# Two of the six channel sums in the first image's spectral mixings: on TensorE with the identity and a ScalarE copy, instead of a VectorE reduction

## The chip, the cores and the metric

The kernel runs on one core of one Trainium2 chip. The metric is device microseconds of one execution of the whole program. A core has a matrix engine (TensorE, PE in the profile; its weight loads are listed apart, as PEld), three elementwise engines (VectorE or DVE, ScalarE or ACT, GpSimd or POOL) and queues for transfers, of which SyncE (SP) issues most here. TensorE reads the on-chip memory SBUF and writes accumulator banks (PSUM) of 128 partitions by 512 f32 numbers; VectorE and ScalarE read both.

## The reference, cut to what matters

Eight images of 8 channels by 256 x 256 pixels, in f32. Each image goes through a group normalisation, a lift to 4 groups of 10 channels, four spectral layers, two pointwise layers and a residual sum, and then a second normalisation with a 3 x 3 dilation. A spectral layer is

```python
xf = jnp.fft.rfft2(x).reshape(Bb, G, WID, Hh, Wf)            # G = 4, WID = 10
lo = jnp.einsum('bgixy,gioxy->bgoxy', xf[:, :, :, :M1, :M2], w1c)   # M1 = M2 = 12
hi = jnp.einsum('bgixy,gioxy->bgoxy', xf[:, :, :, Hh - M1:, :M2], w2c)
out_ft = out_ft.at[:, :, :, :M1, :M2].set(lo)
out_ft = out_ft.at[:, :, :, Hh - M1:, :M2].set(hi)
h1 = jnp.fft.irfft2(out_ft, s=(Hh, Ww))
h = swish(h1 + gconv1x1(h))                                  # no swish in the last layer
```

Only 24 x 12 frequencies are kept. At each of them and in each group, ten complex input channels `i` are multiplied by a complex weight and summed into ten output channels `o`. This product and sum over `i` is the mixing, and the change is in its sums.

## The kernel before, in words

One image after the other is worked on, and in each the layers 0 to 3. Of a layer the order is: the spectrum of the layer's input (`spectrum_x` for layer 0, `spectrum_h` for the others), the mixing (`mix`), the rows of the inverse transform (`rows_even`, `rows_odd`), and then `layer`, which goes through eleven chunks of the image: each `burst` adds the inverse transform along the columns and the pointwise convolution in a bank, ScalarE takes it through the swish into `h`, and VectorE and TensorE (`turn`, `transform`, `gather`) already make the forward transform for the next layer. The pointwise layers at the end of an image (its head: `first`, `second`) are cut into 128 steps, which are set between the pieces of the next image's layers at the places where the generators `yield` a text such as "fc". In the first image there is no head to put there: its `mix` runs with nothing between. Layer 0 of the next image is prepared by the generator `start(b + 1)` while layer 3 of this one runs; for the first image it runs ahead of all else.

The order of instructions on TensorE, VectorE, ScalarE and SyncE is the order of the program's text (a manual schedule); each engine works its queue in that order, and a framework adds semaphore waits where one engine needs another's data or its buffer. So an instruction that waits holds up all that stand behind it on the same engine.

In `mix` the partitions are frequencies (24 rows by 4 sets, in 128 partitions) and three values of `k` cover the rest. There are 12 steps, n = 0 to 11: `k = n // 4`, and `k2` is 0 for the real and 1 for the imaginary part of the spectrum. At an even n VectorE multiplies (L420) the weights `sw[k]`, 4 groups x 20 (ten outputs, real and imaginary) x 10 input channels, by the spectrum `bt`, and writes 800 products a partition into `pr`. At an odd n it sums (L423) the ten input channels of each into 80 numbers of `S0` or `S1`. `pr` lies in the third plane of the buffer `turned`, in one half for k2 = 0 and in the other for k2 = 1, so n = 2, 6 and 10 write the same half. When all twelve are done, L438 (odd layers) or L441 and L442 (even layers) form the real and imaginary differences and sums `fs`. TensorE folds these (L464) into the banks of `ps_four`, VectorE copies them to `fz`, and TensorE makes the rows (L496 in even layers, L518 in odd ones), which ScalarE (L215) and VectorE (L217) copy to `zt` for the bursts.

Accumulator banks come from two tags: "one" (`ps_a`, one bank, two buffers in turn) and "tri" (three banks, two buffers). The weights of the three `k` are loaded by the SP queue (L409) into three buffers `sw`, those of the next layer as soon as this layer's multiplications have freed them; in layer 3 the next image's x is loaded by the same queue at n = 2 (L78). `ident` is a 128 x 128 identity that the kernel already has for its transposes (L324).

Other lines that are spoken of: L318 and L331, matmuls of the first image's spectrum, the second with a full 128 x 128 weight; L325 and L334, the VectorE copies before and after L331; L390 and L401, the matmuls of `spectrum_h`; L600, L603 and L606, the matmuls of a burst (L600 in layer 0, where the input has 6 rows of each 32; L603 in the other layers).

Of the kernel before, what the change touches and what calls it, by code (L numbers as in the profile page):

```python
# [12 lines left out]
AF = mybir.ActivationFunctionType  # L13
# [9 lines left out]
WID = 10  # L23
# [23 lines left out]
def fno_dilate_kernel(ctx: ExitStack, tc: tile.TileContext, a: dict, out: bass.AP):  # L47
    nc = tc.nc
    mm = nc.tensor.matmul
# [9 lines left out]
    def ps_a(name):  # L59
        return ps.tile([128, 512], F32, tag="one", bufs=2, name=name)  # L60

    def ps_tri(name):
        return ps.tile([128, 3, 512], F32, tag="tri", bufs=2, name=name)

    def ps_four(name):
        one, tri = ps_a(f"{name}_0"), ps_tri(f"{name}_1")
        return one, tri, [one] + [tri[:, i, :] for i in range(3)]

    def part(i):
        return slice(32 * i, 32 * i + 32)  # L70
# [5 lines left out]
    def load_x(b):  # L76
        for i in range(2):
            nc.sync.dma_start(turned[:, i], a["xw"][b, :, i])  # L78
# [10 lines left out]
    ident = const.tile([128, 128], F32, tag="ident", name="ident")  # L89
# [79 lines left out]
    p = ps_tri("p_wc")  # L169
    for g in range(G):  # L170
        mm(p[32 * g : 32 * g + 6, 0, :32], fc0x[part(g), :], wt[part(g), 0, g, :], start=True, stop=True)
    for i in range(2):
        for r in range(4):
            mm(p[part(r), 1, NO * G * i : NO * G * (i + 1)], fc0c[:, i, :], wbd[:, NO * r : NO * (r + 1), :],
               start=True, stop=True)
# [236 lines left out]
    def mix(b, l, out_):  # L412

        s = [sb.tile([128, 3, 2, WID, G], F32, tag=f"S{i}", bufs=1, name=f"S{i}_{b}_{l}") for i in range(2)]
        bt, sw = out_["bt"], out_["sw"]
        for n in range(12):
            k, k2 = n // 4, n // 2 % 2
            pr = turned[:, 2, 1024 * k2 : 1024 * k2 + 800].rearrange("p (g m i) -> p g m i", g=G, i=WID)
            if n % 2 == 0:
                nc.vector.tensor_tensor(  # L420
                    pr, sw[k], bt[:, k2, k].unsqueeze(2).to_broadcast([128, G, 2 * WID, WID]), ALU.mult)
            else:
                nc.vector.tensor_reduce(  # L423
                    s[k2][:, k].rearrange("p s o g -> p (s o) g"),
                    pr.rearrange("p g m i -> p m g i"), AX.X, ALU.add,
                )
            if l == 0:
                if n % 2:
                    yield
            elif n not in (0, 2, 6, 10):  # L430
                yield {1: "fc", 4: "fC", 7: "fC", 9: "fC"}.get(n, "f")
            if n == 2 and l == 3 and b + 1 < n_img:
                load_x(b + 1)
        for i, (x, y, op) in enumerate((
                (s[0][:, :, 0], s[1][:, :, 1], ALU.subtract), (s[0][:, :, 1], s[1][:, :, 0], ALU.add),
                (s[1][:, :, 1], s[0][:, :, 0], ALU.subtract))):
            if l % 2:
                nc.vector.tensor_tensor(fs2[:, :, i].rearrange("p g k o -> p k o g"), x, y, op)  # L438
                continue
            three = [t[:, :, :9].rearrange("p k (r o) g -> p k r (o g)", r=3) for t in (x, y)]  # L440
            nc.vector.tensor_tensor(fs[:, 0:3, i].rearrange("p r k o g -> p k r (o g)"), *three, op)  # L441
            nc.vector.tensor_tensor(fs[:, 3, i, :, 0], x[:, :, 9], y[:, :, 9], op)  # L442
        yield "fc"

        if l % 2:
            src, cols = fs2.rearrange("p g i k o -> p g i (k o)"), fz2
            nc.vector.memset(fz2[:, :, 25], 0.0)
            if l == 1:
                nc.vector.tensor_copy(fz2[:, :, 24], cz1)
            else:  # L450
                nc.vector.memset(fz2[:, :, 24], 0.0)
        else:
            src, cols = fs.rearrange("p r i k o g -> p r i (k o g)"), fz.rearrange("p o g c -> p (o g) c")
            if l == 2:
                nc.vector.tensor_copy(fz[:, :, :, 24], cz[:, 1])
                nc.vector.memset(fz[:, :, :, 25], 0.0)
            else:
                nc.vector.tensor_copy(fz[:, :, :, 25], cz[:, 2])
        n_f = 6 * cols.shape[1]
        one, tri, banks = ps_four(f"p_f_{b}_{l}")  # L460
        for term in range(2):
            for r in range(4):
                for q in range(4):
                    mm(banks[q][part(r), :n_f], fold[part(q), term, :],  # L464
                       src[part(q), r, term : term + 2].rearrange("p t x -> p (t x)"),
                       start=term == 0, stop=term == 1)
        if l == 0:
            mr = out_["mr"]
            nc.vector.tensor_tensor(dc[:, 0:1], mr[:, 0:1], mr[:, 1:2], ALU.mult)
            out_["wcn"] = sb.tile([128, 32], F32, tag="wcn", bufs=1, name=f"wcn_{b}")  # L470
            nc.vector.tensor_scalar(out_["wcn"], wc, mr[:, 1:2], None, ALU.mult)
            for r in range(4):
                mm(one[part(r), n_f : n_f + NO * G], dc, wm[:, NO * r : NO * (r + 1), :], start=True, stop=True)
        nc.vector.tensor_copy(
            cols[:, :, 6:24].rearrange("p x (q c) -> p q c x", q=3),
            tri[:, :, :n_f].rearrange("p q (c x) -> p q c x", c=6))
        nc.vector.tensor_copy(
            cols[:, :, 0:6].rearrange("p x c -> p c x"), one[:, :n_f].rearrange("p (c x) -> p c x", c=6))
        if l == 0:
            nc.vector.tensor_tensor(  # L480
                fz[:, :, :, 24], one[:, n_f : n_f + NO * G].rearrange("p (o g) -> p o g", o=NO), cz[:, 0], ALU.add)
# [204 lines left out]
    def start(b, out_):  # L686
        if b < n_img:
            if b == 0:
                out_["sw"] = [load_sw(0, k) for k in range(3)]
            yield from spectrum_x(b, out_)  # L690
            yield from mix(b, 0, out_)
# [11 lines left out]
    def layers(b, stored, d, then, ahead):  # L703

        for l in range(4):
            if l > 0:
                yield from spectrum_h(b, l, d)  # L710
                yield from mix(b, l, d)
            yield from rows_odd(b, l, then) if l % 2 else rows_even(b, l)
            yield from layer(b, l, d, stored, then, ahead)
        yield "stored"
        yield from rest(b, then)
# [429 lines left out]
```

## Time and profile before

| | |
|---|---|
| median of 3 runs | 3658.42 us (3650.33, 3658.42, 3659.02) |
| profiled execution | 3659.15 us, its span 3657.4 us |
| mean granted TensorE clock | 0.977 of full |
| busy: TensorE, ScalarE, VectorE | 3478.5, 2873.7, 2381.7 us |
| L420, products, 192 of them | 188.7 us, 983 ns each |
| L423, sums, 192 of them | 188.9 us, 984 ns each |
| the first image's four mixings (n = 0 to 11) | from 40.45, 123.40, 199.49 and 277.07 us, 11.6 us each |

The 192 products and 192 sums are those of 32 mixings (8 images, 4 layers). The span is the time from the first to the last instruction of one profiled execution; all times in the trace count from its start. A line of the profile gives start and length in us, engine, line in the code, operation, output <- inputs, shape, and in brackets how long the engine had been idle before it and what ended that. A line by source gives the shortest, median and longest duration of the line's instructions in ns.

### The profile page before, as it was taken

How to read it: one execution, taken by the hardware profiler on the slowest of the kernel's cores; microseconds unless marked ns; L12 is line 12 of the kernel's file. 1: busy time of each engine (PE TensorE's matmuls, PEld its weight loads, DVE VectorE, ACT ScalarE, POOL GpSimd, SP SyncE). 2: the span in 40 equal slices, each digit the busy share in tenths (PEclk: the TensorE clock that was granted, in tenths of full speed). 3: DMA queues.
4: the chain of work that ended last, by engine and by line, in shares of the span. 5: the costliest groups of instructions: out<-in, count | busy, mean ns of one | idle time of the engine just before them, and what ended most of it. 6: DMA issues, size and time to landing. Idle time of an engine off the chain costs nothing.

```text
span 3657.4 us, 112630 instructions
## 1 busy us (share of the span) xinstructions
PE 3478.5 (95%) x50872; PEld 1271.2 (35%) x50872; DVE 2381.7 (65%) x3697; ACT 2873.7 (79%) x3035; POOL 117.0 (3%) x202
## 2 busy tenths in 40 slices
PE   5768999999999999999999999999999999999997
PEld 2323333333333333333333333333333333333222
DVE  6776656557775677756776577766777567772443
ACT  2435888888888888887888888888888888889986
POOL 1000000000000000000000000000000000000000
PEclk7878999999999999999999999999999999999998
DMA  3005211442225222271223512254222521225331
GB/s 93 16 15 206 58 47 50 152 121 65 76 87 185 81 60 73 87 226 55 64 60 126 183 56 76 64 166 119 67 76 87 192 81 53 71 70 191 83 84 48
DMA packets 114080, 344.70 MB, mean 94 GB/s; under 512 B 15985, under 2 KB 18481, under 8 KB 98177
## 3 DMA queue, kind: packets, MB, share of 16 engines
q1 hardware_dynamic: 95392, 276.32, 24.9%
q0 software_dynamic: 18208, 61.18, 5.3%
q8 instruction: 400, 6.55, 0.7%
q14 instruction: 80, 0.65, 0.1%
HBM read 213.44 MB, written 123.74 MB: 92 GB/s over the span
## 4 chain that ended last, share of the span: by engine, by line
PE 80%; DVE 13%; ACT 4%; issue 3%; DMA 0%; ACTq 0%; DVEq 0%; POOL 0%; POOLq 0%
PE p_fc L825 21%; PE p_fc L842 21%; PE p_z L606 10%; PE p_d L567 8%; PE p_z L603 8%; PE p_u L585 3%; PE p_z L600 3%; DVE y L851 2%; DVE S L423 2%; DVE turned L420 2%; DVE turned L550 2%; PE p_b L390 1%; DVE turned L381 1%; PE p_g L518 1%; ACT act L826 1%
## 5 line engine op out<-in xcount | busy, mean ns | idle before, releaser
L827 ACT ACTIVATE act<-p_fc 128x1536 f32<-128x1536 f32 x1024 | 1492.0, 1457 | 3.1 <-PE p_fc L825 3.1
L825 PE MATMUL p_fc<-hs,c_w 32*128 32x512 f32 x8192 | 1132.7, 625 | 24.6 <-DVE y L851 10.0
L842 PE MATMUL p_fc<-act,c_w 128*32 128x512 f32 x8192 | 1007.1, 599 | 0.5 <-ACT act L827 0.2
L826 ACT ACTIVATE act<-p_fc 128x512 f32<-128x512 f32 x1024 | 616.0, 602 | 199.7 <-PE p_fc L825 187.6
L550 DVE STREAM_TRANSPOSE turned<-h 128x1024 f32<-128x1024 f32 x528 | 632.6, 1226 | 196.0 <-ACT h L611 195.2
L611 ACT ACTIVATE h<-p_z 128x512 f32<-128x512 f32 (+1 forms) x528 | 512.0, 1021 | 205.8 <-PE p_z L606 205.8
L851 DVE TENSOR_TENSOR y<-p_fc,y 128x512 f32<-128x512 f32 x392 | 267.7, 683 | 526.0 <-PE p_fc L842 526.0
L825 PEld LDWEIGHTS p_fc<-hs,c_w 32*128 32x128 f32 x8192 | 357.9, 184 | 595.0 <-ACT act L826 260.2
L842 PEld LDWEIGHTS p_fc<-act,c_w 128*32 128x32 f32 x8192 | 222.4, 109 | 704.9 <-issue 327.4
L606 PE MATMUL p_z<-c_binv,zt 32*128 32x256 f32 x5632 | 414.2, 408 | 0.1
L606 PEld LDWEIGHTS p_z<-c_binv,zt 32*128 32x128 f32 x5632 | 261.2, 188 | 309.5 <-issue 296.1
L603 PE MATMUL p_z<-h,c_wt 32*32 32x512 f32 x8448 | 358.0, 601 | 7.9 <-ACT act L826 4.2
L567 PE MATMUL p_d<-turned,c_fw 32*32 32x480 f32 (+1 forms) x9216 | 308.0, 539 | 0.6 <-DVE turned L550 0.2
L575 ACT ACTIVATE turned<-p_d 128x1440 f32<-128x1440 f32 x144 | 183.1, 1272 | 89.7 <-PE p_d L567 86.6
L613 ACT ACTIVATE h<-p_z,c_bias 128x512 f32<-128x512 f32 (+1 forms) x176 | 186.6, 1111 | 72.0 <-PE p_z L606 71.8
L215 ACT ACTIVATE zt<-p_g 128x198 f32<-128x198 f32 (+2 forms) x132 | 62.5, 583 | 177.6 <-PE p_g L496 93.7
L423 DVE TENSOR_REDUCE S<-turned 128x80 f32<-128x800 f32 x192 | 188.9, 984 | 5.9
L420 DVE TENSOR_TENSOR turned<-t,B 128x800 f32<-128x800 f32 x192 | 188.7, 983 | 1.1
L567 PEld LDWEIGHTS p_d<-turned,c_fw 32*32 32x32 f32 x9216 | 127.5, 103 | 165.5 <-issue 63.8
L381 DVE STREAM_TRANSPOSE turned<-zt 128x960 f32<-128x960 f32 x96 | 177.1, 1868 | 2.5
L603 PEld LDWEIGHTS p_z<-h,c_wt 32*32 32x32 f32 x8448 | 92.9, 103 | 175.5 <-DVE y L851 48.8
L585 PE MATMUL p_u<-turned,c_stack 128*32 128x480 f32 (+1 forms) x1152 | 136.7, 543 | 7.2 <-DVE turned L574 6.2
(198 smaller groups left out, 1748.2 us busy)
## 6 DMA issues: line engine op xcount, KB each, us to landing
stored<-h SPq DMA_DIRECT2D x88, 1024.0 KB
hs<-stored SPq DMA_DIRECT2D x352, 256.0 KB
t<-in_spw SPq DMA_DIRECT2D x96, 400.0 KB
yin<-y_rows POOLq DMA_DIRECT2D x56, 512.0 KB, 5.1
h<-in_xp SPq DMA_DIRECT2D x352, 48.0 KB
turned<-in_xw SPq DMA_DIRECT2D x16, 1024.0 KB
y<-in_x SPq DMA_DIRECT2D x56, 256.0 KB
y_rows<-y POOLq DMA_DIRECT2D x56, 256.0 KB, 3.9
```

Of the source, the lines that this page charges most:

```text
L420: nc.vector.tensor_tensor(pr, sw[k], bt[:, k2, k].unsqueeze(2).to_broadcast([128, G, 2 * WID, WID]), ALU.mult)
L423: nc.vector.tensor_reduce(s[k2][:, k].rearrange("p s o g -> p (s o) g"), pr.rearrange("p g m i -> p m g i"), AX.X, ALU.add,)
L550: nc.vector.transpose(dst[:, 2 * i : 2 * i + 2], h[:, c, 2 * i : 2 * i + 2].rearrange("p f (s x) -> p f s x", s=2))
L567: mm(banks[q][part(v % 4), : 240 * n], fw8[part(q), v, :], t[part(q), :, :, v, : NBLK * WID], start=v < 4, stop=v >= 4)
L603: mm(o, wt[part(q), l, g, :], h[part(q), c, f, :], start=True, stop=False)
L606: mm(banks[q][:, HW * s : HW * (s + 1)], zt[part(q), 2 * c + s].rearrange("p f o -> p (f o)"), binv[part(q), :], start=False, stop=s == 1)
L611: nc.scalar.activation(dst, src, AF.Silu)
L825: mm(banks[g], w1[part(g), blk, :], hs[k][part(g), :], start=True, stop=True)
L826: nc.scalar.activation(act[:, 0, :], one, AF.Silu)
L827: nc.scalar.activation(act[:, 1:4, :], tri, AF.Silu)
L842: mm(acc[part(g), :], w2[:, g, 15 - rb - i : 47 - rb - i], act[:, g, :], start=i == 0, stop=i == 1)
L851: nc.vector.tensor_tensor(y, sums, y, ALU.add)
```

## The change

Where the image is the first (b = 0), in each of its four layers, the sums at n = 3 and n = 7 (k2 = 1, k = 0 and 1) are no longer made by VectorE. TensorE takes a bank of tag "one" and multiplies the identity, as the stationary weight, by the 80 products of input channel i, for i = 0 to 9, accumulating in the bank; so the bank holds the sum over i. The ten matmuls read `pr` with i fixed, in the order (output, group): successive numbers are 800 bytes apart in g (4 of them) and 40 bytes apart in m (20 of them). ScalarE then copies the 80 numbers to the same place in `S1`. The other four sums of these mixings, and all sums of the other images, stay on VectorE.

```diff
             if n % 2 == 0:
                 nc.vector.tensor_tensor(
                     pr, sw[k], bt[:, k2, k].unsqueeze(2).to_broadcast([128, G, 2 * WID, WID]), ALU.mult)
+            elif b == 0 and n in (3, 7):
+                p = ps_a(f"p_mix_{b}_{l}")
+                for i in range(WID):
+                    mm(p[:, 0:80], ident, pr[:, :, :, i].rearrange("p g m -> p m g"), start=i == 0, stop=i == WID - 1)
+                nc.scalar.activation(
+                    s[k2][:, k].rearrange("p s o g -> p (s o g)"), p[:, 0:80], AF.Copy)
             else:
                 nc.vector.tensor_reduce(
                     s[k2][:, k].rearrange("p s o g -> p (s o) g"),
```

## The prediction

> **What bounds the kernel now.** I read the page first: TensorE (PE) is busy 95% of the span and carries 80% of the chain that ended last. The granted clock in forty slices shows where the change lies: only the first four slices (366 us) and the last are below 9 tenths, and the first image fills nearly those.
>
> ```profile
> PE 3478.5 (95%) x50872; PEld 1271.2 (35%) x50872; DVE 2381.7 (65%) x3697; ACT 2873.7 (79%) x3035; POOL 117.0 (3%) x202
> PEclk7878999999999999999999999999999999999998
> ```
>
> The average says nothing about the first image: there is no earlier image whose head could fill its mixings. So I read the timeline of one of them (layer 1):
>
> ```profile
> 124.42 0.99 DVE L423 TENSOR_REDUCE S<-turned 128x80 f32<-128x800 f32 x1
> 125.33 0.98 DVE L420 TENSOR_TENSOR turned<-t,B 128x800 f32<-128x800 f32 x1
> 126.34 0.99 DVE L423 TENSOR_REDUCE S<-turned 128x80 f32<-128x800 f32 x1
> 127.25 0.98 DVE L420 TENSOR_TENSOR turned<-t,B 128x800 f32<-128x800 f32 x1
> 128.26 0.99 DVE L423 TENSOR_REDUCE S<-turned 128x80 f32<-128x800 f32 x1
> 129.17 0.98 DVE L420 TENSOR_TENSOR turned<-t,B 128x800 f32<-128x800 f32 x1
> ```
>
> VectorE works without a gap, one operation each 0.96 us; of its step n=2 (125.33) the sum n=3 follows at 126.34, and n=6 starts at 129.17. Then the windows of the four mixings (PE, PE loads, VectorE, ScalarE, GpSimd, then granted clock), and of two stretches after them:
>
> ```profile
> 40.45:52.10 11.65, 0.00 (x0) 0.00 (x0) 11.40 (x13) 0.00 (x0) 0.00 (x0) 0.50 0.43 106
> 123.40:135.04 11.64, 0.00 (x0) 0.00 (x0) 11.40 (x12) 0.00 (x0) 0.00 (x0) 0.50 0.23 72
> 277.07:288.71 11.64, 0.00 (x0) 0.00 (x0) 11.40 (x12) 0.00 (x0) 0.00 (x0) 0.50 0.33 139
> 58.39:72.04 13.65, 13.65 (x179) 4.88 (x176) 5.42 (x5) 7.93 (x9) 0.00 (x0) 0.50 0.01 2
> 136.89:140.31 3.42, 2.72 (x104) 2.75 (x112) 1.43 (x4) 0.00 (x0) 0.00 (x0) 0.50 0.02 5
> ```
>
> Two things: VectorE alone sets the mixing's 11.6 us (PE's fold, L464, waits 12.8 us for it), so what is gained or lost there goes straight to the end. And PE stands at half clock in it.
>
> **What a group of the new matmuls costs.** The nearest rows are L331, also a full 128x128 weight, in a stretch at full clock, and L496, 128 weight columns at half clock:
>
> ```profile
> L331 PEld LDWEIGHTS p_a<-c_fw,turned x8: 186/192/192, 34.4 to 35.2; 128*128 128x128 f32 x8
> L331 PE MATMUL p_a<-c_fw,turned x8: 269/269/290, 34.4 to 35.2; 128*128 128x24 f32 x8
> 34.40 0.97 PEld L331 LDWEIGHTS p_a<-c_fw,turned 128*128 128x128 f32 x8 [1.02 <-DVE turned L325]
> 34.41 1.07 PE L331 MATMUL p_a<-c_fw,turned 128*128 128x24 f32 x8 [0.78 <-DVE turned L325]
> L496 PEld LDWEIGHTS p_g<-c_rowg,fz x20: 281/328/332, 54.6 to 57.4; 32*128 32x128 f32 x20
> ```
>
> Four calls in the code leave eight loads and eight matmuls: an f32 matmul is two of each. The eight loads start every (970-192)/7 = 111 ns although each must be followed by its matmul: the loads set the pace, the matmuls hide under them. [...] At half clock a load goes from 186 to 281 ns, 95 more. So a load paces at 111+95 = 206 to 2x111 = 222 ns; I take 215. [...] L390's 48 matmuls of 120 columns, four side by side, took 2.63 us at half clock, 12 rounds of about 200 ns[...]. Our 80 columns then stream in 133 ns cold (67 warm), under the load either way.
>
> A group of ten calls is 20 loads and 20 matmuls: cold 19 x 0.215 + a tail. The tail is 0.29 us for L331 (1.07 - 7 x 0.111); cold and with 80 columns for 24 it grows by 0.10 (load) and 0.11 (133 less 20 ns of stream) to 0.50. G = 4.09 + 0.50 = 4.6 us. Warm: 19 x 0.111 + 0.34 = 2.46 us.
>
> **Is it cold?** [...] being busy isn't enough: from 58.39 to 72.04 PE was busy all the time and stayed at 0.50. There L600 feeds only 6 of each 32 rows. [...] The window from 136.89, mostly L518 at all rows, [...]ended the half clock. The group streams 133 of each 215 ns[...]. I take cold.
>
> **The sum.** Removed, per mixing: two sums of 0.99 us at n=3 and n=7. Added: two groups, and a wait that the diff doesn't show: n=2, n=6 and n=10 write the same half of `turned`, so n=6 waits until the group has read it, and n=10 for the second. Behind n=6 on VectorE everything queues, the fold on PE too. From the end of n=2 (126.31) to n=6 (129.17) it was 2.86 us. Now: 0.05 hand-over to PE (34.35 to 34.40 at L325 to L331) + 4.6 + 0.04 back (35.48 to L334 at 35.51) = 4.69; meanwhile VectorE does n=4 and n=5 in 1.95 us and stands idle 2.7. So +1.83 us a group, eight groups (two in each of four layers): +14.6 us. Bounds: 2.55 warm gives -0.31 a group, -2.5 in all; the strided read below gives +23.6.
>
> Hidden: the copies on ScalarE. Its row for 198 elements is 583 ns on average, so 80 take less; ScalarE has no other work before L215, and n=10 and n=11 (1.95 us) cover the last copy; without that cover it is 0.4 us at most in each mixing. The bank is one of the pair "one", whose earlier readers ended before n=0, and the fold takes it after the copy, much later. ScalarE's function loads keep their number and their place. The loads on the SP queue (next layer's weights, the x of the second image) are issued at the same steps and landed long before their use (x by 282 for 296.7). Nothing in the trace between 52 and 300 us waits for a transfer that would absorb the shift, so all of it passes to the end. The profiled execution was 3659.15 us (span 3657.4), 0.7 above the median: 3659.15 + 14.6 = 3673.8, and from the median 3658.42, 3673.0.
>
> **Rivals.**
> *The clock rises.* If the weight loads count as activity, the first group brings the full clock. For it: PE would be busy without a break for over 4 us. Against it: L606 loads as densely and the bursts at 58 to 72 stayed cold. Groups of 2.46 us: 3655.9. If the clock also held over the 2.7 us from the second group to the fold, layer 0's four bursts would go from 3.98 to 2.24 us (1.09+1.15 as later), another -7.0: 3649, on the other side of no change. The point from which it decides is a group of 2.77 us: shorter gains, longer loses.
> *The strided read slows PE.* The moving columns lie 40 and 800 bytes apart. [...] L390, which reads runs of three, took 2.63 us cold and 1.96 warm, not half; isolated elements are in no row. At 267 ns a matmul, twice the stream, G is 19 x 0.267 + 0.65 = 5.7, +2.95 x 8 = +23.6: 3682. At 200 ns nothing changes cold, but a warm group is then 4.2 us, +11: 3669.
> *It is swallowed.* The runs of before lie at 3650.3 and at 3658.4 to 3659.0. The trace has one window of 3.4 us at half clock in layer 0 of each of the last six images (the first from 788.84 to 792.25), after L600 with its six rows[...]. At up to 1.7 us each, six are up to 10, the size of that step. A luckier phase could give 8 us back: 3665, or with a smaller group 3660.
>
> **How the numbers follow.** Cold, paced by loads: 0.57, 3673, own range 3664 to 3677. Strided read: 0.15, 3669 to 3682. Clock rises: 0.16, 3649 to 3669. Swallowed, 0.12, 3656 to 3665. 0.3% is 11 us, about what a measurement of this kernel can tell from no change. Slower than 3669.4: nearly all of the first, less a tenth, and most of the second, 0.66. Faster than 3647.4: only the full clock with its carry and a lucky phase, 0.06. Same: 0.28. The range 3656 to 3681 leaves out the carry and the worst stride.
>
> **What would show it.** In the changed profile: ten calls as 20 loads, 4.6 us from the first load to the last matmul's end; VectorE idle about 2.7 us before n=6 and n=10, released by PE; each mixing 15.3 us instead of 11.6; clock 0.50 in it. Wrong would be a group below 2.8 us, loads nearer than 200 ns, or a clock of 1.00 in the second group.

## The result, and the profile after

The changed kernel took 3673.6 us in the median of six runs (3667.0 to 3677.1), the kernel before 3658.7 in six runs beside it; the ratio is 1.0042, with a 95% interval from 1.0031 to 1.0052. That is 15 us more. One execution on record is left out of the ratios of this text: 7457 us, of the kernel below with idle matmuls ahead of the mixing. The profiled execution took 3672.47 us, with a span of 3670.7 us for 3657.4 before.

The page's busy times, the granted clock in forty slices, and the products' row among the costliest groups, which is new there in one thing, its idle time:

```profile
PE 3514.0 (96%) x51032; PEld 1306.4 (36%) x51032; DVE 2374.3 (65%) x3689; ACT 2875.5 (78%) x3043; POOL 117.0 (3%) x202
PEclk7887999999999999999999999999999999999998
L420 DVE TENSOR_TENSOR turned<-t,B 128x800 f32<-128x800 f32 x192 | 188.2, 984 | 23.2 <-PE p_mix L425 22.1
```

VectorE lost eight sums (3697 to 3689 instructions) and is busy 7.4 us less, TensorE is busy 35.5 us more, and the products now stand idle for 22.1 us in front of TensorE's new line: eight waits of 2.8 us. The timeline of the same mixing as shown before (layer 1; the change puts in L425 and L426, so that the lines behind them have numbers six higher than before: the sums are L429, the fold is L470):

```profile
130.25 1.88 DVE L420 TENSOR_TENSOR turned<-t,B 128x800 f32<-128x800 f32 x2
131.35 4.34 PEld L425 LDWEIGHTS p_mix<-turned,ident 128*128 128x128 f32 x20 [4.37 <-issue]
131.38 4.52 PE L425 MATMUL p_mix<-turned,ident 128*128 128x80 f32 x20 [3.57 <-DVE turned L420]
132.17 0.99 DVE L429 TENSOR_REDUCE S<-turned 128x80 f32<-128x800 f32 x1
135.94 0.24 ACT L426 ACTIVATE S<-p_mix 128x80 f32<-128x80 f32 x1 [21.30 <-PE p_mix L425]
135.94 1.89 DVE L420 TENSOR_TENSOR turned<-t,B 128x800 f32<-128x800 f32 x2 [2.79 <-PE p_mix L425]
136.99 4.55 PE L425 MATMUL p_mix<-turned,ident 128*128 128x80 f32 x20 [1.08 <-DVE turned L420]
141.58 0.99 DVE L420 TENSOR_TENSOR turned<-t,B 128x800 f32<-128x800 f32 x1 [2.73 <-PE p_mix L425]
143.70 0.77 DVE L444 TENSOR_TENSOR fs<-S,S 128x120 f32<-128x120 f32 x3
```

The first line holds n=2 and n=4, the sum of n=5 follows at 132.17, and then VectorE waits until 135.94, 2.79 us, until TensorE has read the half of `turned` that n=6 must overwrite. The same again at 141.58 for n=10. From n=0 (128.32) to the subtraction (143.70) it is 15.38 us, where it was 11.64.

The windows of three of the four mixings, from n=0 to 0.07 us ahead of the subtraction, and as the last line one of 3.4 us wholly inside a group (the columns are as in the prediction):

```profile
41.52:56.83 15.31, 9.08 (x40) 8.68 (x40) 9.62 (x10) 0.47 (x2) 0.00 (x0) 0.50 0.32 79
128.32:143.63 15.31, 9.08 (x40) 8.68 (x40) 9.62 (x10) 0.47 (x2) 0.00 (x0) 0.50 0.18 55
289.15:304.46 15.31, 9.08 (x40) 8.68 (x40) 9.62 (x10) 0.47 (x2) 0.00 (x0) 0.50 0.25 106
131.72:135.12 3.40, 3.40 (x18) 3.40 (x17) 1.40 (x2) 0.00 (x0) 0.00 (x0) 0.50 0.35 120
```

PE and its loads have no gap in the last window, and the clock stays at 0.50. In layer 2, not shown, it is 0.57: 1.00 for the first 2.2 us (208.02 to 210.20), and 0.50 from there on, when the groups ran (the first from 211.08).

All four mixings are 3.7 us longer, 14.9 us together. The spans differ by 13.3 us; the rest of that lies outside the mixings. In the profile after, the first product stands 1.1 us later (41.52 for 40.45), before any changed instruction. The stretches between the mixings add less than 0.1 us together, so the second image's layer 0 starts 16.0 us later (341.32 for 325.28); and from there to the end the changed kernel's execution is 2.7 us quicker. From the third on, an image takes 433.4 to 433.6 us where one window at half clock (3.4 us) falls in its layer 0 and 431.9 to 432.2 where none does. Before had such a window in each of the last six images. After had it in two of them, which gives back 5.9 us, but two more in the second image (1.7 us) and one late in the last, at 3514.3 (1.5 us).

### The profile page after: what moved, and what is told of

Same layout as the page of the kernel before. It is cut to its first block, busy times and chain, and to the rows that moved or that the text cites. A ratio compares the mean times of both kernels' runs of the same rounds, so it can differ in the third digit from the quotient of the medians.

```text
span 3670.7 us, 112966 instructions
## 1 busy us (share of the span) xinstructions
PE 3514.0 (96%) x51032; PEld 1306.4 (36%) x51032; DVE 2374.3 (65%) x3689; ACT 2875.5 (78%) x3043; POOL 117.0 (3%) x202
## 4 chain that ended last, share of the span: by engine, by line
PE 80%; DVE 13%; ACT 4%; issue 3%; DMA 0%; ACTq 0%; DVEq 0%; POOL 0%; POOLq 0%
PE p_fc L831 21%; PE p_fc L848 21%; PE p_z L612 10%; PE p_d L573 8%; PE p_z L609 8%; PE p_u L591 3%; PE p_z L606 3%; DVE y L857 2%; DVE turned L420 2%; DVE S L429 2%; DVE turned L556 2%; DVE turned L381 1%; PE p_b L390 1%; PE p_g L524 1%; ACT act L832 1%
## 5 line engine op out<-in xcount | busy, mean ns | idle before, releaser
L420 DVE TENSOR_TENSOR turned<-t,B 128x800 f32<-128x800 f32 x192 | 188.2, 984 | 23.2 <-PE p_mix L425 22.1
L429 DVE TENSOR_REDUCE S<-turned 128x80 f32<-128x800 f32 x184 | 181.1, 984 | 5.6
L580 DVE COPY turned<-p_d 128x480 f32<-128x480 f32 x144 | 86.8, 602 | 81.1 <-PE p_d L573 63.3
```

The source lines that it names most:

```text
L420: nc.vector.tensor_tensor(pr, sw[k], bt[:, k2, k].unsqueeze(2).to_broadcast([128, G, 2 * WID, WID]), ALU.mult)
L429: nc.vector.tensor_reduce(s[k2][:, k].rearrange("p s o g -> p (s o) g"), pr.rearrange("p g m i -> p m g i"), AX.X, ALU.add,)
```

## The experiments

Ratios are to the kernel before, run beside each (its median was between 3651.9 and 3658.9 us), with a 95% interval; 0.001 is 3.65 us. "Mixings" is the time from n=0 to the subtraction, of the four layers in the profile, 46.57 us together before and 61.51 after. A kernel's lines move down by what is put in above them.

### One sum of the two

```diff
-            elif b == 0 and n in (3, 7):
+            elif b == 0 and n in (3,):
```

> The changed kernel with the sum at n=3 alone on TensorE; the other five stay on VectorE. Theory (each group costs its wait, one for one): n=6 starts 1.83 us later than before the change and n=10 with it, a mixing takes 13.5 us, half of the loss: 7.3 us more than before. Rival (something is paid once, the first use of bank or engine): a mixing of 15 us, nearly the whole loss; or of 11.6, all of it in the second group.

The ratio is 1.0015 (1.0006 to 1.0024), 5.5 us more. A mixing takes 13.58 us, the four 54.3, which is 7.7 us more than before, half of 14.9. The wait ahead of n=6 is the same 2.79 us, and n=10 has none:

```profile
133.52 0.99 DVE L420 TENSOR_TENSOR turned<-t,B 128x800 f32<-128x800 f32 x1 [2.79 <-PE p_mix L425]
```

So each group costs its wait, one for one, and nothing is paid once.

### A place of their own for the products of n=6

```diff
+        pr2 = sb.tile([128, G, 512], F32, tag="act", bufs=4, name=f"pr_{b}_{l}").rearrange("p g f -> p (g f)") if b == 0 else None
         for n in range(12):
             k, k2 = n // 4, n // 2 % 2
             pr = turned[:, 2, 1024 * k2 : 1024 * k2 + 800].rearrange("p (g m i) -> p g m i", g=G, i=WID)
+            if b == 0 and n in (6, 7):
+                pr = pr2[:, 0:800].rearrange("p (g m i) -> p g m i", g=G, i=WID)
```

The pool "act" belongs to the heads and is free until the first image's end.

> The changed kernel, with the products of n=6 written to a place of their own, so that neither n=6 nor n=10 waits for TensorE to have read. Theory (the loss is VectorE's wait for the buffer): VectorE is through with its ten operations at 9.8 us, the groups run one behind the other from 3.0 to 7.6 and to 12.1 us, the ScalarE copy ends at 12.4, and the subtraction waits for it alone: a mixing takes 12.4 us for 15.3 and 11.6 before, time 3662. Rival (n=6 waits for something else, or TensorE's time counts in full): a mixing stays at 14 us or more, time 3670.

The ratio is 1.0003 (0.9995 to 1.0012), no difference that can be told, and of the 14.9 us in the mixings 2.0 are left. The timeline of layer 1, from the products of n=6 on:

```profile
129.52 0.98 DVE L423 TENSOR_TENSOR pr<-t,B 128x800 f32<-128x800 f32 x1
132.16 4.46 PE L428 MATMUL p_mix<-pr,ident 128*128 128x80 f32 x20
133.41 0.99 DVE L432 TENSOR_REDUCE S<-turned 128x80 f32<-128x800 f32 x1
136.65 0.24 ACT L429 ACTIVATE S<-p_mix 128x80 f32<-128x80 f32 x1 [4.03 <-PE p_mix L428]
136.92 0.77 DVE L447 TENSOR_TENSOR fs<-S,S 128x120 f32<-128x120 f32 x3 [2.52 <-ACT S L429]
```

n=6 starts at 129.52, without a wait (n=0 was at 124.77). TensorE's groups are as long as in the change and follow one another; VectorE is done at 134.40 and waits 2.52 us, once, for ScalarE's copy of the second group. A mixing takes 12.15 us, 0.5 more than before: with two groups TensorE itself is now what ends last.

### Small tiles instead of a full identity

```diff
-                    mm(p[:, 0:80], ident, pr[:, :, :, i].rearrange("p g m -> p m g"), start=i == 0, stop=i == WID - 1)
+                    for q in range(4):
+                        mm(p[part(q), 0:80], stack[part(q), :], pr[part(q), :, :, i].rearrange("p g m -> p m g"),
+                           start=i == 0, stop=i == WID - 1)
```

> The changed kernel, with each of the ten full 128 x 128 identity matmuls cut into four of 32 x 32 on the diagonal (the weight is the 32 x 32 identity that the kernel holds four times). A load then has 32 columns for 128, and the four lie in different rows, side by side. Theory (at half clock the loads set the pace): the loads vanish from the pace, the stream of 2 x 133 ns per channel sets it, a group takes 3.1 us for 4.55, n=6 starts 3.2 us after the end of n=2 for 2.86 before the change, a mixing takes 12.3 us for 15.3, time 3661. Rival (the strided read of the products sets the pace): a channel takes 2 x 190 ns or more, a group 4.2 us, a mixing 14.6 us, time 3670.

The ratio is 1.0010 (1.0001 to 1.0019), 3.7 us more, and the mixings are 4.2 us longer than before. Layer 1:

```profile
128.42 3.18 PE L426 MATMUL p_mix<-turned,c_stack 32*32 32x80 f32 x80 [3.57 <-DVE turned L420]
131.66 1.89 DVE L420 TENSOR_TENSOR turned<-t,B 128x800 f32<-128x800 f32 x2 [1.46 <-PE p_mix L426]
```

The same numbers are read at the same clock with the same strides, only the loads are 32 columns wide and four small matmuls stand for one: a group is 3.18 us for 4.52, and the wait 1.46 for 2.79. So the loads did set the pace, 0.211 us from one to the next ((4.34-0.33)/19). The 80 matmuls are 20 rounds of four; with a last one of 0.32 us a round is (3.18-0.32)/19 = 0.150 us.

The same layer's second group ran at another clock. It was 0.50 from 128.42 to 131.60 and 1.00 from 132.70 to 135.30:

```profile
132.70 3.16 PE L426 MATMUL p_mix<-turned,c_stack 32*32 32x80 f32 x80 [1.11 <-DVE turned L420]
```

It took 3.16 us, as long as the first. So what paces the tiles is not the stream at half clock that the theory had (2 x 133 ns a channel, 3.1 us, an estimate from L390): that its group came out near is luck.

### Successive numbers instead of strided ones, at half clock

```diff
-                    mm(p[:, 0:80], ident, pr[:, :, :, i].rearrange("p g m -> p m g"), start=i == 0, stop=i == WID - 1)
+                    mm(p[:, 0:80], ident, pr.rearrange("p g m i -> p (g m i)")[:, 80 * i : 80 * i + 80],
+                       start=i == 0, stop=i == WID - 1)
```

> The changed kernel with the ten matmuls reading 80 successive products each (the sums are then not those over the channels, which this leaves out), at half clock as in the change. Theory (the loads set the pace at half clock, the read is hidden under them): groups of 4.55 us as in the change, mixings of 15.3 us. Rival (the strided read has a part in the half-clock group): shorter groups.

```profile
132.03 4.53 PE L425 MATMUL p_mix<-turned,ident 128*128 128x80 f32 x20 [3.56 <-DVE turned L420]
```

The groups take 4.53 and 4.56 us and the mixings 61.5 us, as in the change (4.52 and 4.55): at half clock the read is under the loads. This kernel has a single execution, so its groups are compared and not its time.

### The clock brought up ahead of the mixing

```diff
+        if b == 0:
+            w = ps_a(f"p_warm_{b}_{l}")
+            for _ in range(3 if l == 0 else 2):
+                mm(w, ident, wt.rearrange("p l g o -> p (l g o)"), start=True, stop=True)
         for n in range(12):
```

Two kernels: this with the change as it is, and this with the successive reads of the edit above.

> The changed kernel, with idle matmuls (128 x 512, into a bank that nobody reads) ahead of each mixing of the first image, three in layer 0 and two in the others, to bring the clock to full before the first group. Theory (half clock makes the group long): at 1.00 a group takes 2.5 us (a load each 111 ns), VectorE's wait for it is 0.6 us for 2.7, a mixing takes 11.0 us, time 3656 or less if TensorE stays at full clock after it. Rival (the strided read sets the pace as soon as the loads don't): a group takes about 4.2 us at full clock also, a mixing 14.5 us, time 3670. If the clock stays at 0.50, neither is tested.

> As the run with idle matmuls ahead of the mixing, but the ten matmuls read 80 successive products each (the sums are then not those over the channels, which this leaves out). Theory: at full clock the same group of 2.5 us as with strided reads, since the loads set the pace in both. Rival (strided reads are slower): the group takes 2.5 us here and about 4.2 us there.

In layer 2 the clock was 1.00 when both groups began, in both. By source, first with the strided reads of the change, then the timeline of its groups:

```profile
L429 PEld LDWEIGHTS p_mix<-turned,ident x40: 186/210/333, 210.1 to 217.5; 128*128 128x128 f32 x40
210.14 3.23 PE L429 MATMUL p_mix<-turned,ident 128*128 128x80 f32 x20 [1.66 <-DVE turned L424]
214.45 3.56 PE L429 MATMUL p_mix<-turned,ident 128*128 128x80 f32 x20 [1.08 <-DVE turned L424]
```

And the same with successive reads:

```profile
L429 PEld LDWEIGHTS p_mix<-turned,ident x40: 186/192/192, 206.3 to 211.9; 128*128 128x128 f32 x40
206.29 2.43 PE L429 MATMUL p_mix<-turned,ident 128*128 128x80 f32 x20 [1.66 <-DVE turned L424]
209.81 2.46 PE L429 MATMUL p_mix<-turned,ident 128*128 128x80 f32 x20 [1.08 <-DVE turned L424]
```

With successive reads a group at full clock takes 2.43 us, close to the 2.46 that the prediction had for it, and layers 1 to 3 have mixings of 11.2 to 11.3 us (layer 0, which fell back to half clock at 45.4, has 14.6). With the strided reads it takes 3.23: a matmul each (3.23-0.33)/19 = 0.153 us, nearly the same as a round of the tiles at either clock, 0.150. So the strided read has a pace of its own, 0.150 to 0.153 us for a matmul's 80 columns, the same at 0.50 and at 1.00; the loads hide it at half clock (211 ns from one to the next) and not at full clock (111 ns, by 20 loads in 2.31 us with successive reads). Neither theory had the size: the one expected 2.5 us, the rival 4.2. The second group of the strided kernel fell back to half clock on the way (its loads reach 333 ns), and in layers 0, 1 and 3 the second group ran at half clock throughout, 4.55 us; those mixings are 14.1 to 14.8 us. The ratio of the strided kernel is 1.0023 (1.0014 to 1.0031), 8.4 us more than before; the other kernel has a single execution.

### The clock alone

The kernel before, with idle matmuls spread over the mixing:

```diff
+            if b == 0 and n in (1, 3, 5, 7, 9):
+                w = ps_a(f"p_warm_{b}_{l}_{n}")
+                mm(w, ident, pr.rearrange("p g m i -> p (g m i)")[:, 0:512], start=True, stop=True)
             if l == 0:
```

> The kernel before the change (all six sums on VectorE), with one idle matmul of 512 columns, into a bank that nobody reads, over the products of each of the first five pairs of steps in the first image's mixings. It asks what the half clock costs by itself. Theory: [...]the mixing stays at 11.6 us, the fold begins at 1.00, and layer 0's four bursts go from 4.0 to 2.2 us (-7), the rows and first bursts of layers 1 to 3 gain 2 to 3 us each: 15 us less than before, 3637. Rival (the clock falls again before the fold, or TensorE isn't what those stretches wait for): within 3 us of before, 3649 to 3655.

The ratio is 1.0002 (0.9993 to 1.0011), no difference. The windows of layer 0's mixing from 46.9 and of the bursts after it:

```profile
46.90:53.80 6.90, 3.29 (x76) 1.46 (x76) 6.38 (x17) 0.00 (x0) 0.00 (x0) 0.99 0.39 128
53.90:74.40 20.50, 20.13 (x241) 8.39 (x245) 9.71 (x11) 10.54 (x14) 0.00 (x0) 0.50 0.01 2
```

The idle matmuls did bring the clock to full (0.50 from 43.5 to 46.9, then 0.99), and it fell again at 53.9, before the bursts, over a fold of 0.9 us and a wait of 2.4 us ahead of it. The four bursts ran at half clock, as before. In layers 1 to 3 it fell too, at 135.84, 210.93 and 289.44, within 2 us after the mixing's end (134.10, 210.72 and 288.06). So the theory of this run is wrong much as its rival has it: the clock falls again, in layer 2 before the fold and in layer 0 right after it. What the bursts would gain at full clock wasn't tried.

### The groups early, with places of their own

`pr2` is made as for the place of n=6.

```diff
+            if b == 0 and n > 3:
+                pr = pr2[:, 1024 * k2 : 1024 * k2 + 800].rearrange("p (g m i) -> p g m i", g=G, i=WID)
...
-            elif b == 0 and n in (3, 7):
+            elif b == 0 and n in (1, 3):
```

> The changed kernel with the two groups at n=1 and n=3 instead of 3 and 7, and the products from n=4 on in places of their own, so that no step waits for TensorE and the two groups have the whole mixing before them. Theory (a group is 4.55 us at half clock, and only its wait was dear): groups from 1.1 to 5.6 and to 10.2 us, the copy at 10.5; a mixing takes 10.5 us for 11.6 before the change: 4.5 us less than before, 3647. Rival (the sums on TensorE cost something besides the wait): a mixing of 11.6 us or more, no gain.

The ratio is 0.9979 (0.9968 to 0.9989): 7.7 us faster than before the change. The mixings take 40.9 us, 5.7 less. Layer 1:

```profile
125.30 8.80 PE L428 MATMUL p_mix<-turned,ident 128*128 128x80 f32 x40 [1.65 <-DVE turned L423]
134.13 0.24 ACT L429 ACTIVATE S<-p_mix 128x80 f32<-128x80 f32 x1 [4.03 <-PE p_mix L428]
134.40 0.77 DVE L447 TENSOR_TENSOR fs<-S,S 128x120 f32<-128x120 f32 x3 [0.67 <-ACT S L429]
```

The same two groups of the same length at the same half clock, 40 matmuls in a row now, and VectorE waits 0.67 us once. The same with the small tiles:

> The same with the four 32 x 32 identities for the full one. Theory: groups of 3.2 us end at 4.3 and 7.5, under VectorE's ten operations; a mixing takes 9.7 us, that is 2.0 less than before the change, two sums: 7.8 us less than before, 3644. Rival as above: no gain.

The ratio is 0.9985 (0.9978 to 0.9992), 5.5 us faster than before. Here no wait is left:

```profile
121.93 6.14 PE L429 MATMUL p_mix<-turned,c_stack 32*32 32x80 f32 x160 [1.65 <-DVE turned L423]
130.47 0.77 DVE L449 TENSOR_TENSOR fs<-S,S 128x120 f32<-128x120 f32 x3
```

A mixing takes 9.68 us, the four 38.7, 7.9 less than before: two sums of VectorE each, as expected. That the run time shows 5.5 of it, with an interval from 2.9 to 8.0, is not more than the half-clock windows can scatter; this profile has one in layer 0 of five of the last six images, that of the full identity in none.

### One sum early, and the clock

The edits are those of the tiles, of the places of their own and of the idle matmuls over the mixing.

> One sum in tiles at n=1 (its products left alone, later ones in places of their own), and idle matmuls as in the run on the clock alone after n=3, 5, 7 and 9. Theory: a mixing takes 10.7 us (one sum less), and the clock is full at the fold: 4 and 15 us less than before, 3633. If the clock does not hold, 3648.

The ratio is 0.9986 (0.9977 to 0.9995), 5.1 us faster, not the 19 of the theory, and near the 3648 that it had for a clock that does not hold (the median is 3648.6). In the run on the clock alone it did not hold; then only the sum is left. Its profile shows mixings of 11.0 us in layers 1 and 2 and 11.7 in layers 0 and 3, where a product waited 0.9 us for an idle matmul that was still reading; by that execution the mixings gain 1.2 us, less than the interval's near end of 1.8. What makes up the rest isn't settled.

### The mixings and the runs together

| kernel | mixings less 46.57 us | from the ratio (interval), us |
|---|---|---|
| the change | +14.9 | +15.4 (11.3 to 19.0) |
| one sum | +7.7 | +5.5 (2.2 to 8.8) |
| clock ahead of the mixing | +9.6 | +8.4 (5.1 to 11.3) |
| tiles | +4.2 | +3.7 (0.4 to 6.9) |
| own place for n=6 | +2.0 | +1.1 (-1.8 to 4.4) |
| clock alone | 0.0 | +0.7 (-2.6 to 4.0) |
| early | -5.7 | -7.7 (-11.7 to -4.0) |
| early, tiles | -7.9 | -5.5 (-8.0 to -2.9) |
| one sum early, and clock | -1.2 | -5.1 (-8.4 to -1.8) |

What the mixings gain or lose goes to the end, within the intervals, in all but the last row.

## Why the prediction was right, by its steps

- *The load's pace.* 215 ns was taken, between 206 and 222. The 20 loads span 4.34 us, the last 0.33 long: (4.34-0.33)/19 = 211 ns between starts. The tiles showed that it is the loads (3.18 us a group for 4.52). The upper bound, twice the 111 ns of full clock, was the sound one; the lower took the shortest load of L496 (281 ns) for a load's time, and with that line's median, 328, it would have been about 250. The stream set beside it, 133 ns and 67 at full clock, was an estimate: L390's 200 ns for 120 columns, taken to 80 and then halved. At full clock the strided read took 153.
- *The group.* 4.6 us predicted, 4.55 measured from the first load to the last matmul's end.
- *The wait.* 2.7 us idle ahead of n=6 and n=10 predicted, 2.79 and 2.73 measured. In layer 1 n=2 ends at 131.24 (130.25 and 0.99 us), the first load starts at 131.35 and n=6 at 135.94: 4.70 us for the 4.69 predicted. The hand-over to TensorE is 0.11 us, twice what was taken, and the group a little shorter. The run with a place of its own showed that it is the buffer's wait: without it 2.0 us of the loss are left while the groups are as long as before.
- *The mixing.* 15.3 us predicted, 15.38. The sum was 14.6, it is 14.9: of the rest, 0.07 us a mixing is a longer step from the last sum to the subtraction (142.61 to 143.70, 1.09 us, for 134.02 to 135.04, 1.02 us), 0.28 in all, and what is left is rounding.
- *The copy.* At most 0.4 us, hidden: 0.24 us, and only where VectorE no longer covers it (own place, early) does it stand on the path.
- *Half clock.* 0.50 in all but the first 2.2 us of layer 2's mixing (0.57 in its window). That the groups would not end the half clock was an estimate, by its 133 of each 215 ns, and it came out so. Before the change the clock went from 0.50 to 1.00 at 140.31, behind the prediction's window with L518, in which TensorE was busy for 2.72 of 3.42 us. The run with the groups early says most plainly that busy time does not do it: TensorE had no gap for 8.80 us from 125.30 (40 loads in 8.61 us), and the clock stayed at 0.50 there and in the other three layers. With the tiles, in layer 1, TensorE stood idle for 3.57 us and was then busy for 3.18, and the clock rose at 131.93, 0.33 us after that. What decides it was not shown.

Of the rivals, *the clock rises* was wrong for this kernel, and its price was half right: 2.43 us for a group, but only with successive reads; the carry of 7 us into the bursts did not come when the clock was raised on purpose. *The strided read* is real and was mis-sized: 0.150 to 0.153 us a matmul at either clock, not 0.267, so it hides under the loads here (0.211). *It is swallowed* happened in part: the half-clock windows gave 2.7 us back in the profiled execution, not 8.

That the median came out at 3673.6 for the 3673.0 predicted is partly luck: single executions of the changed kernel lie 10 us apart, as much as six of those windows come to at 1.6 us each. The mixing, 15.38 us for 15.3, and the wait in it don't depend on them.

## What to carry to other kernels

An engine that is idle is not free of charge: price the moved work at the clock that it will get there (0.50 here), and then ask who waits for its reading, not only for its result. Here the result was wanted late and the input's buffer soon; giving the products a place of their own and starting the groups first turned 15 us lost into 6 to 8 won (by the mixings and by the ratio), with the same matmuls on TensorE. And where each matmul brings its own weight, ask whether the load sets the pace. At half clock it did: four 32 x 32 identities side by side do in 3.2 us what the full one does in 4.5.

## What the runs showed that was not expected

TensorE read single f32 numbers, 40 and 800 bytes apart, at one pace at half clock and at full clock: 3.18 and 3.16 us for a group in tiles, 0.150 us a round, and 0.153 us a matmul with the full identity at full clock. Successive ones took 2.43 us a group at full clock, at the loads' pace (111 ns). And an execution's time depends on how many images have a half-clock window in their layer 0: about 1.6 us for each (433.5 for 431.9 us). Of the last six images all had one before the change, two after it, and none and five in the two early kernels. By the 1.6 us, an estimate, six come to nearly 10 us of the scatter that a change of this size has to be seen through.
